# Two chained layers in float32: other loads at the head, and a planner that counts GpSimd's DMAs

## The chip, the cores and the metric

The kernel runs on one core of a Trainium2 chip. The metric is device time in microseconds; of several executions the median is taken. TensorE (PE) does the matmuls, VectorE (DVE) additions and transposes, ScalarE (ACT) scaling and copies, GpSimd (POOL) issues DMAs and SyncE (SP) issues most loads.

## The reference

Eight sequences x[b] of 256 rows by 1024 go through two layers, each added to its input. The first layer is one linear layer plus a masked term; the second picks one of eight weight matrices by an index per sequence:

```python
y = x + (x @ W.T + bias) + (x @ (2 * mask[b] - 1)) * coeff[b]   # mask[b]: 1024 x 1024 of int32
out = y + y @ weight[ids[b]].T                                  # weight[...]: 1024 x 1024
```

All is float32. The mask is 4 MB per sequence, as is the chosen weight. In the first layer both products share x, so the kernel forms one matrix, W.T + coeff * (2 * mask - 1), and multiplies once.

## The kernel before, in words

**Stages.** Layer and sequence make a stage: (0,0), (1,0), (0,1), (0,2), (1,1), (0,3) and so on, 16 in all. Stage (0,0) is the head and is written apart. Every other stage multiplies a 256x1024 by a 1024x1024 matrix with seven block products (Winograd's form of Strassen's scheme): x and the weight are cut into 2x2 blocks, sums s1 to s4 and t1 to t4 are made by DVE (lines 530 and 547), and seven products of 128x512 by 512x512 go into PSUM (line 596; stage 1, which yields the transposed result, uses line 586). Results are added into a buffer r in SBUF by DVE (line 660), some by way of a copy by ACT (line 632).

In a stage of layer 0, each of four mask blocks (1 MB, line 494) is scaled by ACT (`2c * mask - c`, line 503) and folded with W by DVE (line 517). Buffer r begins as the rows of x (line 397), to which a GpSimd DMA adds the bias in flight (line 407). The result is transposed by DVE (line 427) and moved by ACT (line 441) for the second layer. Layer 1 loads its weight blocks from the address that the index gives (line 499); SP reads the index at line 497. Results are stored by GpSimd's queue (line 686). Eleven weight buffers of 1 MB circulate, so a load waits until a buffer is free.

**The head.** Sequence 0 has its 1024 input features in eight groups of 128, k = 0 to 7. For each k, SP loads 128 rows of the mask (`load_mask`, line 267) and of W (`load_w0`, line 274), 512 KB each; k=0 and k=1 come in two column halves (`pieces`, line 248), so there are ten pieces n. Loads of x for this sequence (`load_x0`, line 261; 128 KB per k) go between them in four parts: k=0, k=1, k=2..3, k=4..7. ACT scales a piece (`scale_first`, line 290), DVE adds W (`fold_first`, line 298), and PE multiplies (`mm_first`, line 305), 16 matmuls of 128x256 per k. Piece 0 is scaled and folded in two parts of 256 columns (`parts`). At the end ACT makes x + bias (`bias_first`, line 323) and DVE evicts the four PSUM banks (`evict_first`, line 332). The stage after it starts when these are done.

Three loads of the head, W's first piece (line 785), the index (786) and the coefficients (784), are issued on ACT's queue, and the bias in a layout by partitions (line 278) too, with piece 4. Nine idle matmuls run before the first real one.

**What sets the order.** The order of the whole program is made at build time. Each step is a `Task` with an engine, an estimated length, the tasks it follows, the buffers it takes, and `latest`, a time by which it should start. `plan` is a list scheduler: going through time, it starts on each free engine the ready task with the earliest `latest`. All loads are tasks of one resource "DMA"; stores and bias adds are tasks of POOL, with a length on POOL and a latency. Tasks are then emitted by planned start; every engine runs its own list in that order and waits for the real completions. The estimates are the constants in lines 46 to 48 (PRODUCT is a block product, BLOCK a DVE operation on 128x2048, SMALL one on 128x512, SCALE a mask block on ACT, SHUFFLE a move of line 441), and `HEAD`, 34.5, is where the plan expects the head to end.

Of the kernel before, what the change touches and what calls it, by code (L numbers as in the profile page):

```python
# [14 lines left out]
P = 128  # L15
# [27 lines left out]
}  # L43


PRODUCT, BLOCK, SMALL = 3.435, 2.29, 0.69
SCALE, COPY, SHUFFLE = 2.10, 0.60, 0.42
LOAD, STORE, LATENCY, BEGIN = 2.50, 0.60, 2.2, 1.7


class Task:
    def __init__(
        self, engine, length, emit, after=(), takes=(), uses=(), latency=0.0, latest=None, earliest=0.0
    ):
        self.earliest = earliest
        self.engine, self.length, self.emit = engine, length, emit
        self.after = [t for t in after if t is not None]
        self.takes, self.latency, self.latest = takes, latency, latest
        self.uses = list(takes) + list(uses)
        for r in self.uses:  # L60
            r.users += 1
        self.start = self.end = None
# [9 lines left out]
def plan(tasks, room, may_take):  # L72

    followers = {t: [] for t in tasks}
    for t in tasks:
        for u in t.after:
            followers[u].append(t)
    for t in reversed(tasks):
        due = [f.latest for f in followers[t]]
        own = t.latest + t.length if t.latest is not None else 1e9  # L80
        t.latest = min(due + [own]) - t.length - t.latency
    waiting = {t: len(t.after) for t in tasks}
    ready = {}
    for t in tasks:
        ready.setdefault(t.engine, [])
        if not waiting[t]:
            ready[t.engine].append(t)
    free_at = dict.fromkeys(ready, 0.0)
    free_at["DMA"] = BEGIN
    left = {}  # L90
    events, now, done = [(BEGIN, None)], 0.0, 0
    while done < len(tasks):
        for engine, queue in ready.items():
            if free_at[engine] > now + 1e-9:
                continue
            for t in sorted(queue, key=lambda t: t.latest):
                if t.earliest > now + 1e-9:
                    events.append((t.earliest, None))
                elif all(room[r.pool] > 0 for r in t.takes) and may_take(t):
                    queue.remove(t)  # L100
                    for r in t.takes:
                        room[r.pool] -= 1
                        left[r] = r.users
                    t.start, t.end = now, now + t.length + t.latency
                    free_at[engine] = now + t.length
                    events += [(t.end, t), (free_at[engine], None)]
                    break
        assert events, "the plan is stuck"
        now = min(e[0] for e in events)
        for e in [e for e in events if e[0] <= now + 1e-9]:  # L110
            events.remove(e)
            t = e[1]
            if t is None:
                continue
            done += 1
            for r in t.uses:
                left[r] -= 1
                if not left[r]:
                    room[r.pool] += 1
            for f in followers[t]:  # L120
                waiting[f] -= 1
                if not waiting[f]:
                    ready[f.engine].append(f)
    order = {t: i for i, t in enumerate(tasks)}
    return sorted(tasks, key=lambda t: (round(t.start, 6), order[t]))
# [3 lines left out]
def kernel(  # L129
# [26 lines left out]
    nc = tc.nc  # L156
    B = coeff.shape[1]
    _, _, _, KH, TH = xT.shape
    NL, _, _, _, H = w1T.shape
    KC, D = 2 * KH, 2 * H  # L160
# [84 lines left out]
    first = {(j, h): Buffer("ps") for j in range(2) for h in range(2)}  # L245
    xb = Buffer("r")
    half = KH // 2
    pieces = [(k, ds(j * H, H)) for k in range(2) for j in range(2)]
    pieces += [(k, ds(0, D)) for k in range(2, KC)]
    w0_rows = w0_sb.rearrange("p k j n -> p k (j n)")  # L250

    def x0_view():
# [10 lines left out]
    def load_mask(n: int):  # L263
        k, cols = pieces[n]
        if m[k // 2].tile is None:
            take(m[k // 2])
        nc.sync.dma_start(out=m_view(k)[:, cols].bitcast(I32), in_=mask0[k][:, cols])  # L267
        if n == 0:
            load_x0(0, 1, nc.sync)

    def load_w0(n: int):
        k, cols = pieces[n]
        if n:
            nc.sync.dma_start(out=w0_rows[:, k, cols], in_=w0T[k][:, cols])  # L274
        if n in (1, 3, 5):
            load_x0(*{1: (1, 2), 3: (2, KH), 5: (KH, KC)}[n], nc.sync)
        if n == 4:
            nc.scalar.dma_start(out=b_sb, in_=biasT)

    def parts(n: int):  # L280
        k, cols = pieces[n]
        if n:
            return k, [cols]
        return k, [ds(cols.start, cols.size // 2), ds(cols.start + cols.size // 2, cols.size // 2)]

    def scale_first(n: int):
        k, spans = parts(n)
# [54 lines left out]
    for n, (k, cols) in enumerate(pieces):  # L342
        share = cols.size / D
        opens = opened != k // 2
        length = 1.25 * share if n else 0.4
        ld = task(
            "DMA",
            1.32 * share,
            lambda n=n: load_mask(n),
            takes=[m[k // 2]] if opens else [],  # L350
            uses=[] if opens else [m[k // 2]],
            latency=1.5,
            latest=0.2 * n,
        )
        ld2 = task(
            "DMA", 1.32 * share, lambda n=n: load_w0(n), latency=1.5, latest=0.2 * n + 0.1
        )
        sc = task("ACT", length, lambda n=n: scale_first(n), after=[ld], uses=[m[k // 2]])
        fo = task("DVE", length, lambda n=n: fold_first(n), after=[sc, ld2], uses=[m[k // 2]])
        folded.append(fo)  # L360
        last_scale = sc
        opened = k // 2
        if n == 0:
            tasks[0].takes = [x0] + list(tasks[0].takes)
            tasks[0].uses = [x0] + list(tasks[0].uses)
            x0.users += 1
# [26 lines left out]
    def load_r(b: int, begin: float):  # L393
        task_ = task(
            "DMA",
            LOAD,
            lambda: nc.sync.dma_start(
                out=take(R[b]), in_=xR[b - 1].rearrange("p t (j n) -> p (t j) n", n=H)
            ),
            takes=[R[b]],  # L400
            latency=LATENCY,
            earliest=begin - 8 * PRODUCT,
        )
        return task(
            "POOL",
            1.2,
            lambda: nc.gpsimd.dma_start(  # L407
                out=R[b].tile.rearrange("p (t j) n -> p t (j n)", t=2),
                in_=bias.to_broadcast((P, D)).unsqueeze(1).to_broadcast((P, 2, D)),
                accum_op=ALU.add,  # L410
            ),
            after=[task_],
            uses=[R[b]],
            latency=6.0,
        )

    def turn(j: int, source, after, target: Buffer, opens: bool, view, moved: list):
# [39 lines left out]
    def stage(s: int):  # L457
# [222 lines left out]
        def store(q: str, cols, queue=None):  # L680
            j = int(q[1]) - 1
            lo, hi = j * H + cols.start, j * H + cols.stop
            task(
                "POOL",
                STORE,
                lambda: (queue or nc.gpsimd).dma_start(  # L686
                    out=out0[:, block(q)] if flipped else out[b - 1, :, int(q[0]) - 1, lo:hi],
                    in_=R[b].tile[:, block(q), cols],
                ),
                after=[state[q]],  # L690
                uses=[R[b]],
                latency=3.0,
            )

        copies: dict[str, tuple] = {}
# [86 lines left out]
    with tc.manual_schedule():  # L782
        take(x0)
        nc.scalar.dma_start(out=c_row, in_=coeff)  # L784
        nc.scalar.dma_start(out=w0_rows[:, 0, pieces[0][1]], in_=w0T[0][:, pieces[0][1]])
        nc.scalar.dma_start(out=ids_sb, in_=ids)
        v.memset(zeros, 0.0)
        v.memset(ones, 1.0)
        v.memset(warm, 0.0)

        nc.scalar.activation(warm, warm, AF.Identity, bias=warm, scale=1.0)
        idle = pools["ps"].tile([P, H], F32, tag="ps", name="idle")
        c_ps = pools["ps"].tile([P, B], F32, tag="ps", name="c_ps")
        for n in range(9):
            nc.tensor.matmul(out=idle, lhsT=zeros[:, 0:P], rhs=zeros, start=True, stop=True)
            if n == 4:
                nc.tensor.matmul(out=c_ps, lhsT=ones, rhs=c_row, start=True, stop=True)
                v.tensor_scalar(c2_sb, c_ps, 2.0, None, ALU.mult)
                v.tensor_scalar(cn_sb, c_ps, -1.0, None, ALU.mult)
        for t in plan(tasks, room, may_take):  # L800
            t.emit()
    if DUMP:
        for t in sorted(tasks, key=lambda t: t.start):
            print("PLAN %s %.2f %.2f %.2f" % (t.engine, t.start, t.end, t.latest))
# [55 lines left out]
```

## Time and profile before

| | |
|---|---|
| Time, median of 3 runs | 407.18 us (405.79 to 408.87) |
| The profiled execution's own time | 409.01 us |
| Its span | 407.2 us |
| PE busy in the span | 396.0 us, 97% |
| DVE busy | 329.9 us, 81% |
| ACT busy | 183.4 us, 45% |
| HBM traffic | 94.38 MB read, 8.39 MB written |

The profile is of one execution; 1.8 us of its time lie around the span. A row of waits reads: engine and line, `<-` and what released it, the total in us, the times, the longest. PEld is the loading of PE's stationary operand, which goes on beside the matmuls; a "q" behind an engine is its sequencer, which issues DMAs. In tables by stretches of the span, PEclk is the clock granted to PE, as a share of the full one. "L298" is line 298 of the kernel before.

### The profile page before, as it was taken

How to read it: one execution, taken by the hardware profiler on the slowest of the kernel's cores; microseconds unless marked ns; L12 is line 12 of the kernel's file. 1: busy time of each engine (PE TensorE's matmuls, PEld its weight loads, DVE VectorE, ACT ScalarE, POOL GpSimd, SP SyncE). 2: the span in 40 equal slices, each digit the busy share in tenths (PEclk: the TensorE clock that was granted, in tenths of full speed). 3: DMA queues.
4: the chain of work that ended last, by engine and by line, in shares of the span. 5: the costliest groups of instructions: out<-in, count | busy, mean ns of one | idle time of the engine just before them, and what ended most of it. 6: DMA issues, size and time to landing. Idle time of an engine off the chain costs nothing.

```text
span 407.2 us, 3451 instructions
## 1 busy us (share of the span) xinstructions
PE 396.0 (97%) x1155; PEld 201.6 (50%) x1155; DVE 329.9 (81%) x304; ACT 183.4 (45%) x303; POOL 25.9 (6%) x42
## 2 busy tenths in 40 slices
PE   7699999999999999999999999999999999999996
PEld 4488996443444444444444444444444444444443
DVE  2235999799998998989999898789997899778142
ACT  4234642221992069422966912585128830292000
POOL 0000022001000110001000101001010010001101
PEclk9899999999999999999999999999999999999999
DMA  7999999998872769928599656958679493611102
GB/s 240 362 413 419 423 397 334 348 368 309 208 310 103 283 232 245 375 76 336 207 261 380 215 191 228 334 249 295 244 174 386 154 391 112 241 68 52 53 0 104
DMA packets 18950, 102.99 MB, mean 253 GB/s; under 512 B 2356, under 2 KB 2868, under 8 KB 9460
## 3 DMA queue, kind: packets, MB, share of 16 engines
q1 hardware_dynamic: 14112, 86.97, 54.7%
q0 software_dynamic: 4384, 15.47, 14.6%
q10 hardware_dynamic: 436, 0.33, 0.3%
q8 instruction: 9, 0.15, 0.1%
q14 instruction: 9, 0.07, 0.0%
HBM read 94.38 MB, written 8.39 MB: 252 GB/s over the span
## 4 chain that ended last, share of the span: by engine, by line
PE 87%; DVE 4%; ACT 4%; DMA 3%; issue 1%; SPq 0%; ACTq 0%; DVEq 0%
PE ps L596 75%; PE ps L586 6%; PE ps L305 6%; DMA w_sb<-w0T 3%; ACT a L441 3%; DVE w L547 2%; DVE w L517 1%; DVE r L660 0%; DVE a L530 0%; DVE w L298 0%; ACT u L632 0%; SPq L267 0%; ACTq L784 0%; SPq L274 0%; SPq L261 0%
## 5 line engine op out<-in xcount | busy, mean ns | idle before, releaser
L596 PE MATMUL ps<-w,a 128*128 128x512 f32 (+1 forms) x792 | 337.2, 588 | 1.1 <-DVE a L530 0.7
L596 PEld LDWEIGHTS ps<-w,a 128*128 128x128 f32 x792 | 149.7, 190 | 188.5 <-issue 183.3
L547 DVE TENSOR_TENSOR w<-w,w 128x2048 f32<-128x2048 f32 (+1 forms) x61 | 136.8, 2249 | 7.6 <-PE ps L596 7.2
L441 ACT ACTIVATE a<-turn 32x256 f32<-32x256 f32 x224 | 92.7, 414 | 33.2 <-DVE turn L427 30.5
L503 ACT ACTIVATE w<-w,cn_sb,c_sb 128x2048 f32<-128x2048 int32 x28 | 58.3, 2091 | 21.4 <-DMA w<-mask 20.8
L517 DVE TENSOR_TENSOR w<-w,w_sb 128x2048 f32<-128x2048 f32 x28 | 63.6, 2280 | 4.9 <-ACT w L503 4.9
L660 DVE TENSOR_TENSOR r<-r,ps 128x512 f32<-128x512 f32 x73 | 49.5, 680 | 18.1 <-PE ps L596 17.4
L632 ACT ACTIVATE s<-ps 128x512 f32<-128x512 f32 x15 | 8.9, 592 | 89.6 <-PE ps L596 80.5
L530 DVE TENSOR_TENSOR a<-a 128x512 f32<-128x512 f32 x59 | 39.1, 680 | 0.6 <-ACT a L441 0.5
L305 PE MATMUL ps<-a,w 128*128 128x256 f32 x128 | 29.8, 397 | 5.6 <-DVE w L298 5.6
L686 POOL DMA_DIRECT2D out<-r x31 | 17.5, 565 | 241.0 <-DVE r L660 241.0
L305 PEld LDWEIGHTS ps<-a,w 128*128 128x128 f32 x128 | 25.3, 199 | 10.2 <-DVE w L298 6.5
L632 ACT ACTIVATE u<-ps 128x512 f32<-128x512 f32 x15 | 9.0, 597 | 43.7 <-PE ps L596 43.6
L298 DVE TENSOR_TENSOR w<-w,w_sb 128x1024 f32<-128x1024 f32 (+2 forms) x11 | 10.2, 933 | 18.8 <-DMA w_sb<-w0T 14.1
L586 PE MATMUL ps<-a,w 128*128 128x128 f32 x192 | 21.8, 275 | 0.0
L586 PEld LDWEIGHTS ps<-a,w 128*128 128x128 f32 x192 | 21.7, 192 | 0.1
L427 DVE STREAM_TRANSPOSE turn<-r 128x512 f32<-128x512 f32 x28 | 19.0, 695 | 0.2
L290 ACT ACTIVATE w<-w,cn_sb,c_sb 128x1024 f32<-128x1024 int32 (+2 forms) x11 | 11.0, 1006 | 17.5 <-DMA w<-mask 16.8
L407 POOL DMA_DIRECT2D r<-bias x7 | 8.7, 1247 | 134.8 <-DMA r<-xR 134.8
L660 DVE TENSOR_TENSOR r<-r,u 128x512 f32<-128x512 f32 x14 | 9.6, 686 | 8.3 <-ACT u L632 8.3
L660 DVE TENSOR_TENSOR r<-r,s 128x512 f32<-128x512 f32 x14 | 9.6, 686 | 6.2 <-ACT s L632 6.1
L332 DVE TENSOR_TENSOR a<-ps,r 128x512 f32<-128x512 f32 x4 | 2.7, 687 | 3.4 <-PE ps L305 3.4
(23 smaller groups left out, 23.4 us busy)
## 6 DMA issues: line engine op xcount, KB each, us to landing
w<-w1T SPq DMA_DIRECT2D x32, 1024.0 KB, 8.2
w<-mask SPq DMA_DIRECT2D x28, 1024.0 KB, 9.3
out<-r POOLq DMA_DIRECT2D x31, 256.0 KB, 5.5
a<-xT SPq DMA_DIRECT2D x7, 1024.0 KB, 11.5
r<-xR SPq DMA_DIRECT2D x7, 1024.0 KB, 13.2
r<-bias POOLq DMA_DIRECT2D x7, 1024.0 KB, 11.3
w<-mask SPq DMA_DIRECT2D x6, 512.0 KB, 9.0
w_sb<-w0T SPq DMA_DIRECT2D x6, 512.0 KB, 9.3
```

The lines of the kernel that those rows point to most:

```text
L305: nc.tensor.matmul(out=t.rearrange("p (c n) -> p c n", c=half)[:, c % half], lhsT=m_view(k)[:, ts(oc, P)], rhs=x0_view()[:, k], start=k == ...
L427: lambda t=t, opens=not turned: v.transpose(out=(take(r) if opens else r.tile)[:, t], in_=view(source.tile)[:, 2 * t + j]),
L441: nc.scalar.activation(to[:, :, :, f], src[:, :, :, g], AF.Copy)
L503: nc.scalar.activation(t, t.bitcast(I32), AF.Identity, bias=cn_sb[:, b : b + 1], scale=c2_sb[:, b : b + 1])
L517: lambda q=q: v.tensor_tensor(W[q].tile, W[q].tile, w0[q], ALU.add),
L530: lambda: v.tensor_tensor(part(what), part(left), part(right), op),
L547: v.tensor_tensor(to[:, rows], a, c, op)
L586: nc.tensor.matmul(out=t[:, ts(c, TH)], lhsT=W[w].tile[:, k, ts(c, P)], rhs=part(a)[:, k], start=opens and c == 0 and k == 0, stop=k == KH ...
L596: nc.tensor.matmul(out=t[:, cols], lhsT=part(a)[:, k], rhs=W[w].tile[:, k, cols], start=opens and k == 0, stop=k == KH - 1, skip_group_che ...
L632: lambda: nc.scalar.activation(take(r), bank.tile, AF.Copy),
L660: v.tensor_tensor(to, left, get(r), op)
L686: lambda: (queue or nc.gpsimd).dma_start(out=out0[:, block(q)] if flipped else out[b - 1, :, int(q[0]) - 1, lo:hi], in_=R[b].tile[:, block ...
```

## The change

It has two parts that are independent in the code.

In the head, W's first piece is loaded by SP like the others, and SP's order becomes mask, W, then x where due, for every piece. Only k=0 is still cut into halves: k=1 is one piece of 1024 columns, so nine pieces are left, and `parts` cuts k=1 for ACT and DVE into halves of 512 columns as before. x comes in three loads: k=0..1, k=2..3, k=4..7. The index and the bias are loaded by GpSimd's queue after the first fold: two memsets on DVE, which these loads must wait for, stand behind it. A tenth idle matmul is added.

In the planner, some of the estimates are set anew, the bias add has a longer latency, and a task can have `moves`: a time for which it holds the resource "DMA" when it starts. Bias adds have 4.0 and stores 0.6.

```diff
-PRODUCT, BLOCK, SMALL = 3.435, 2.29, 0.69
-SCALE, COPY, SHUFFLE = 2.10, 0.60, 0.42
+PRODUCT, BLOCK, SMALL = 3.435, 2.21, 0.61
+SCALE, COPY, SHUFFLE = 2.08, 0.60, 0.425
...
                     free_at[engine] = now + t.length
+                    if t.moves:
+                        free_at["DMA"] = max(now, free_at["DMA"]) + t.moves
+                        events.append((free_at["DMA"], None))
...
-    pieces = [(k, ds(j * H, H)) for k in range(2) for j in range(2)]
-    pieces += [(k, ds(0, D)) for k in range(2, KC)]
+    pieces = [(0, ds(0, H)), (0, ds(H, H))] + [(k, ds(0, D)) for k in range(1, KC)]
...
         nc.sync.dma_start(out=m_view(k)[:, cols].bitcast(I32), in_=mask0[k][:, cols])
-        if n == 0:
-            load_x0(0, 1, nc.sync)
...
-        if n:
-            nc.sync.dma_start(out=w0_rows[:, k, cols], in_=w0T[k][:, cols])
-        if n in (1, 3, 5):
-            load_x0(*{1: (1, 2), 3: (2, KH), 5: (KH, KC)}[n], nc.sync)
-        if n == 4:
-            nc.scalar.dma_start(out=b_sb, in_=biasT)
+        nc.sync.dma_start(out=w0_rows[:, k, cols], in_=w0T[k][:, cols])
+        if n in (0, 2, 3):
+            load_x0(*{0: (0, 2), 2: (2, KH), 3: (KH, KC)}[n], nc.sync)
...
-        if n:
-            return k, [cols]
-        return k, [ds(cols.start, cols.size // 2), ds(cols.start + cols.size // 2, cols.size // 2)]
+        size = {0: 2 * P, 2: H}.get(n, cols.size)
+        return k, [ds(at, size) for at in range(cols.start, cols.start + cols.size, size)]
...
-        length = 1.25 * share if n else 0.4
+        length = {0: 0.4, 2: 0.75}.get(n, 1.22 * share)
...
-            latency=6.0,
+            latency=8.5,
+            moves=4.0,
...
                 latency=3.0,
+                moves=0.6,
...
-        nc.scalar.dma_start(out=w0_rows[:, 0, pieces[0][1]], in_=w0T[0][:, pieces[0][1]])
-        nc.scalar.dma_start(out=ids_sb, in_=ids)
...
-        for n in range(9):
+        for n in range(10):
...
             t.emit()
+            if t is folded[0]:
+
+                v.memset(ids_sb, 0)
+                v.memset(b_sb, 0.0)
+                nc.gpsimd.dma_start(out=ids_sb, in_=ids)
+                nc.gpsimd.dma_start(out=b_sb, in_=biasT)
```

More of the change, by code (lines that the diff above doesn't have):

```diff
@@ L52, in __init__ @@
     def __init__(
-        self, engine, length, emit, after=(), takes=(), uses=(), latency=0.0, latest=None, earliest=0.0
+        self,
+        engine,
+        length,
+        emit,
+        after=(),
+        takes=(),
+        uses=(),
+        latency=0.0,
+        latest=None,
+        earliest=0.0,
+        moves=0.0,
     ):
-        self.earliest = earliest
+        self.earliest, self.moves = earliest, moves
         self.engine, self.length, self.emit = engine, length, emit
```

## The prediction

> **What bounds the kernel now.** I read the page's busy rows first: PE is busy 396.0 us of the 407.2 us span, 97%. A time can only come from the other 11 us, or from PE work at a reduced clock. So I asked next where PE idles, by stretches of the span (columns: length, busy time and count of PE, PEld, DVE, ACT, POOL, granted PE clock, DMA share, GB/s):
>
> ```profile
> 0.00:6.87 6.87, 4.12 (x11) 1.45 (x12) 1.13 (x7) 2.67 (x4) 0.20 (x4) 1.00 0.64 205
> 6.87:14.04 7.17, 7.17 (x32) 5.99 (x32) 2.36 (x4) 2.44 (x3) 0.00 (x0) 1.00 0.86 292
> 14.04:18.07 4.03, 0.01 (x2) 0.00 (x1) 1.23 (x1) 1.28 (x2) 0.00 (x0) 1.00 1.03 413
> 18.07:24.00 5.93, 5.93 (x20) 4.93 (x21) 2.01 (x2) 2.44 (x2) 0.00 (x0) 0.71 1.02 409
> ```
>
> PE does no real product before 6.87, then idles 4.03 us, and afterwards runs at 0.71 of its clock for 5.93 us, which costs 5.93 x 0.29 = 1.7 us. In the head, 128 products need 128 x 0.215 = 27.5 us (3.435 us per k, the code's own figure; the first two k took 7.17 here); they take 33.87, from 6.87 to 40.74. The excess of 6.4 is 4.03 + 1.7 + 0.7.
>
> The waits of PE up to 120 us name the cause, and show how little is lost behind the head:
>
> ```profile
> PE ps L305 <- DVE w L298: 5.6, 2, 4.0
> PE ps L596 <- DVE a L530: 0.7, 1, 0.7
> PE ps L596 <- ACT a L441: 0.4, 1, 0.4
> ```
>
> DVE's fold (L298) is late. The chain that ended last, in order of time, says why:
>
> ```profile
> 1.30 4.96 DMA w_sb<-w0T
> ...
> 8.08 8.62 DMA w_sb<-w0T
> ...
> 16.79 1.24 DVE w L298
> ...
> 18.07 22.67 PE ps L305 x96
> ```
>
> Two loads of w0 set the head: the piece on ACT's queue (issued 1.30, landed 6.26) and the one for k=2 (issued 8.08, landed 16.69). Last, what the DMA engines moved in slices of 1.5 us from 0 to 60, and whom SP waited for up to 45:
>
> ```profile
> GB/s 0 223 169 328 384 385 164 178 348 421 408 426 404 415 407 401 426 401 421 418 426 399 431 426 426 426 426 399 431 426 426 426 426 399 410 426 426 431 415 347
> SPq L274 <- DMA a<-x0T: 3.3, 2, 2.4
> SPq L267 <- DMA w_sb<-w0T: 2.5, 2, 2.1
> SPq L274 <- DMA b_sb<-biasT: 1.8, 1, 1.8
> ```
>
> There are two slumps: 3.0 to 4.5 (169) and 9 to 12 (164, 178). Against 385 they lose 1.5 x 216 = 324 KB and 1.5 x (221 + 207) = 642 KB, 0.8 and 1.7 us of transfer. SP holds loads back until older loads have landed, those of ACT's queue included.
>
> **The change, part by part.**
>
> *Loads.* w0's first piece goes second on SP's queue, x0 comes in three pieces instead of four, and k=1 in two 512 KB loads instead of four of 256 KB; index and bias leave ACT's queue. SP issues mask, w0, x0[0:2], mask, w0 and so on, 0.43 us each. SP gains one issue (the w0 piece) and loses three (two of k=1, one of x0), so its issue never becomes the limit: the first eight loads take about 3.5 us to issue and hold 2.6 MB, nearly 7 us of transfer. Are fewer, larger loads worth something in themselves? The trace says little: the four loads of 256 KB for k=1 landed 0.66 us apart (8.53 to 10.51), 397 GB/s; later ones of 512 KB land 1.28 us apart, 410 GB/s. For 1 MB that is 0.1 us. The Trainium skill (DMA: Bandwidth & Descriptors, [...]Issuing engines are not separate DMA queues) speaks against the other half of the edit: moving DMAs between issuing engines saves only issue time. By that rule the first slump stays and the gain is nothing; the nearest row gives 0.8 us, because the slump begins as ACT's piece starts to move, and SP then waits 2.1 us for its landing. I take 0.8, keeping 0 as the other end.
>
> The second slump (1.7 us) has no operation in the trace that explains it. It starts at 9, before the bias load is issued (9.89), and the loads already issued are far from done. It may be a consequence of the first disorder, of the small loads, or of neither. Ends: 0 and 1.7; I take that it goes, since the fixed order has no second queue there, and the 2 KB pieces of k=1 around it are gone.
>
> *Arrivals.* 0.335 MB are moved by 3.0 us (slice of 223 GB/s from 1.5), then 385 GB/s to k=1 and 410 after. Sums: mask, w0, x0[0:2] 0.79 MB at 4.2; half 1 at 5.5; k=1 at 8.3; x0[2:4] and k=2 at 11.5; x0[4:8] and k=3 at 15.3; then 2.56 per k. The last byte of a load lands later than these sums: before, the loads up to w0 of k=1 (2.36 MB) landed at 10.5, little behind the bytes moved, but those of k=5's mask about 2 us behind. I add 1.0 at the front, 1.5 to 2.0 later. Fold (0.69 per half, 1.23 per k) and PE (3.44 per k) then give: first fold 5.3, first product 5.8, k=0 to 9.25; k=1's first half landed 9.4, folded 10.1, PE 10.1 to 13.55; k=2 landed 13.0, folded 14.25, PE to 17.7; k=3 landed 17.0, folded 18.25, PE to 21.7; from k=4 on (landed 19.9) the loads are ahead. Four more k give 35.5, with 0.2 for stalls 35.7. That is 40.74 - 35.7 = 5.0 us earlier. The gaps are 0.85, 0.7 and 0.55. The skill (TensorE: Matmul & The Clock Gate, Part 1) puts the loss of clock after an idle window of about 3.4 us; the trace has one gap over that, 4.03, and 0.71 behind it. So I count no loss of clock; should gaps of this length cost it too, 1.7 returns.
>
> *Scales and folds.* Part sizes remain 256 or 512 columns for k=0 and k=1; the counts are the same, cost nothing. The tenth idle product costs at most 0.43 (nine end at 5.32); hidden before the first fold at 5.3 to 5.7, otherwise 0.4.
>
> *GpSimd's two DMAs.* Two memsets on DVE (0.06 to 0.27 us by the trace's rows, together about 0.2) stand behind the first fold and ahead of the next, which waits for data anyway. GpSimd's issue waits for them, till about 6; its queue is otherwise empty until 54.59. Landing takes 5.5 us (stores) to 11.3 (the bias adds), so 12 to 18. The index is read on SP at 20.96 now, perhaps 17 then: SP could wait 1 us, with some 4 MB queued behind it in the DMA rings, so nothing starves. ACT needs the bias at about 27 (31.98 now): cover of 9 us.
>
> *The planner.* BLOCK 2.21, SMALL 0.61, SHUFFLE 0.425 are what the trace shows as start to start (2.20, 0.60, 13.60 / 32 = 0.425). A store counts 0.6 us and a bias add 4.0 us of DMA; neither adds an instruction, but the order on SP, DVE and ACT may move anywhere. No row can price that. The bounds: behind the head PE loses 0.70 and about 0.44 us in 65.75 to 115.20, and 363.2 us run against some 361.1 of products (7 of stage 1 in 25.0, 98 x 3.43), so at best -2.1; at worst each 128x2048 block that is wrongly placed before something PE needs costs 2.25, because DVE has no air:
>
> ```profile
> 65.75:93.92 28.17, 27.47 (x65) 11.84 (x64) 26.08 (x23) 6.25 (x6) 2.38 (x3) 1.00 1.01 363
> 93.92:115.20 21.28, 20.84 (x48) 8.96 (x48) 20.87 (x20) 13.74 (x34) 1.19 (x1) 1.00 0.83 258
> ```
>
> I take 0.
>
> *What is late next.* In 66 to 115 DVE is 93% and 98% busy and DMA is full to 92. For PE to run 5.0 earlier, both must. DVE's chain starts with the evictions (36.53), which follow PE, and it holds 2.06 us of waiting for PE at 76.7, so it can follow. DMA is ahead by less: at 25.6 it has moved 9.4 MB instead of some 8.25, 2.9 us; the last mask of batch 2 (ACT waits 5.3 for it, scales at 81.95) has a slack of about 1.7 before DVE comes to it. 2.9 + 1.7 = 4.6; together with roughly half a late block I give back 0.8. Sum: 5.0 - 0.8 = 4.2 us. The profiled execution took 409.01 (1.8 around its span), so 404.8 on its own terms; carried as a difference to the median of the runs shown, 407.18, it is **403.0**. Its execution lies at the upper edge of the runs (405.79 to 408.87), so part of the slump may be its own: a reason for a wide upper side.
>
> **Rivals.** Changes within 1% (403.1 to 411.3) can't be told from none here.
> 1. The head closes and the order is harmless: 403.0 (401.3 to 404.8), chance 0.45, over half of it past 1%.
> 2. The head closes and the truer costs also take away the later waits: 5.0 + 1.5 less, 400.7, chance 0.10. For it: the constants match the trace. Against: only 2.1 us exist.
> 3. The change doesn't do what it says: the slump follows the data, not the queue, as the skill's rule has it. k=2 is then 1.7 to 2.5 late, head end about 38.2, and DMA little ahead; gain about 2, 405.1. If the gap passes 3.4 us the clock takes 1.7 more, 406.5. Chance 0.20. For it: a slump that starts with no operation beside it.
> 4. The head closes, but DVE and DMA give it back by 94 us: 406.5, chance 0.08.
> 5. Slower: the planner's new order. Place: DVE between 65 and 115. Price: 2.25 us per block placed ahead of what PE waits for, 1.7 more once PE idles over 3.4. It decides from the second such block on (4.2 used up), and with the clock passes 1% at three (6.75 + 1.7 - 4.2 = 4.25 over, 411.4); four give 413.7. Chance 0.17.
>
> **Numbers.** Faster by over 1%: 0.28 of case 1, 0.10 of case 2, 0.02 of case 3, together 0.40. Slower: 0.17. Within: 0.43. The range 400.4 to 411.5 leaves out about 0.04 below and 0.16 above; the likeliest case alone has 401.3 to 404.8.
>
> **What would show it.** Right: first product near 5.8, no PE gap over 1.5 us before 20, granted clock 1.00 from 18 to 24, head end near 35.7, PE waits of 1 to 2 us somewhere in 65 to 115. Wrong: slices under 250 GB/s between 4 and 13 us (case 3); PE waiting for DVE blocks in stages 2 to 4 (case 5); or a first product later than 6.9 because ten idle products or x0's 256 KB piece hold it.

## The result, and the profile after

The changed kernel takes 405.64 us (median of 20 runs, 404.37 to 406.61) against 406.97 us for the kernel before (20 runs, 405.63 to 408.87). The ratio is 0.9965, 95% interval 0.9952 to 0.9979: 1.3 us are gained, a third of the 4.2 us forecast. The two profiles are of slow executions: 409.01 us lies above all 20 times of the kernel before, and 406.61 us is the highest of the 20 after.

The stretches of the span again, cut at the same times (kernel after; columns as in the prediction's first table):

```profile
0.00:6.87 6.87, 5.08 (x12) 1.65 (x12) 1.56 (x9) 2.67 (x4) 0.85 (x6) 1.00 0.62 154
6.87:14.04 7.17, 5.48 (x13) 4.43 (x14) 1.99 (x3) 2.33 (x3) 0.57 (x2) 1.00 1.04 406
14.04:18.07 4.03, 4.03 (x19) 3.52 (x19) 1.23 (x1) 1.24 (x1) 0.00 (x0) 1.00 1.02 408
18.07:24.00 5.93, 5.93 (x29) 5.21 (x29) 2.45 (x2) 3.02 (x3) 0.00 (x0) 1.00 1.02 409
```

The gap of 4.03 us is gone, and the clock is 1.00 from 18 to 24 as foretold. But the second row holds 13 products where the kernel before had 32. Two things are in it. PE's first real product starts at 8.56 instead of 6.87. And 13 products fill 5.48 us, 0.42 us each, where the row below has 19 in 4.03, 0.21 each: PE runs at half pace. The clock column shows 1.00 there because it has nothing else to show: the trace's first record of a granted clock is at 14.19. One by one, the products from 9.12 to 13.82 start 0.427 us apart, later ones 0.216.

The chain in order of time (kernel after: start, length, what):

```profile
1.68 6.75 DMA a<-x0T
...
8.56 27.20 PE ps L312 x112
```

The first load of x, issued at 1.68, lands at 8.43; the forecast had 5.2. The same load shows in PE's waits, together with all that PE still waits for behind the head:

```profile
PE ps L312 <- DMA a<-x0T: 2.3, 1, 2.3
...
PE ps L594 <- DVE a L538: 0.2, 1, 0.2
```

What the DMA engines moved, in slices of 1.5 us from 0 to 60 (kernel after):

```profile
GB/s 0 232 197 116 317 403 415 403 408 421 399 412 415 396 418 410 407 429 399 431 421 421 431 410 421 431 421 415 426 415 426 431 410 415 421 415 333 314 306 284
```

Of the two slumps one is left, and it is where it hurts most: 197 and 116 from 3 to 6 us, just when the first product's data should come. From 7.5 us on the stream is full.

So the head ends later than forecast: stage 1's products start at 39.04 (before: 40.58). Behind it the span has 365.8 us left, where the kernel before had 366.6. The stretches in which DVE was thought to have no air (kernel after):

```profile
66.00:94.00 28.00, 28.00 (x66) 12.37 (x66) 27.06 (x23) 8.07 (x6) 1.78 (x2) 1.00 0.89 326
94.00:115.00 21.00, 21.00 (x50) 9.31 (x49) 20.86 (x23) 17.22 (x35) 1.23 (x1) 1.00 0.52 210
```

DVE is still 97% and 99% busy, but PE has no gap any more.

### The profile page after: what moved, and what is told of

The parts are those of the page before. It is cut to its first block, busy times and chain, and to the rows that moved or that the text cites. A ratio compares the mean times of both kernels' runs of the same rounds, so it can differ in the third digit from the quotient of the medians.

```text
span 404.8 us, 3432 instructions
## 1 busy us (share of the span) xinstructions
PE 397.5 (98%) x1156; PEld 203.0 (50%) x1156; DVE 330.6 (82%) x306; ACT 183.5 (45%) x303; POOL 27.2 (7%) x44
## 4 chain that ended last, share of the span: by engine, by line
PE 95%; DMA 2%; DVE 1%; issue 1%; SPq 0%; DVEq 0%
PE ps L604 83%; PE ps L312 7%; PE ps L594 5%; DMA a<-x0T 2%; DVE w L555 1%; DVE a L339 0%; DVE a L538 0%; SPq L283 0%; SPq L279 0%; DVE r L753 0%; DVEq L339 0%
## 5 line engine op out<-in xcount | busy, mean ns | idle before, releaser
L312 PEld LDWEIGHTS ps<-a,w 128*128 128x128 f32 x128 | 26.2, 206 | 7.2 <-issue 3.2
L594 PEld LDWEIGHTS ps<-a,w 128*128 128x128 f32 x192 | 21.8, 192 | 0.5 <-DVE a L538 0.4
```

The lines of the kernel that those rows point to most:

```text
L312: nc.tensor.matmul(out=t.rearrange("p (c n) -> p c n", c=half)[:, c % half], lhsT=m_view(k)[:, ts(oc, P)], rhs=x0_view()[:, k], start=k == ...
L594: nc.tensor.matmul(out=t[:, ts(c, TH)], lhsT=W[w].tile[:, k, ts(c, P)], rhs=part(a)[:, k], start=opens and c == 0 and k == 0, stop=k == KH ...
```

## The experiments

The pitch of x is the distance in DRAM from the start of one of its 128 rows to the start of the next. All ratios are to the kernel before, run on the same chip, where its median was 406.76 to 407.45. "x lands" is the landing of the first load of x (k=0 and 1; with the head of the kernel before k=0 alone, 128 KB), "stage 1" the start of the next stage's products, both in the one profiled execution.

| run | what differs | median us | ratio (95%) | x lands | stage 1 |
|---|---|---|---|---|---|
| before | | 406.97 | 1 | 6.07 | 40.58 |
| after | | 405.64 | 0.9965 (0.9952 to 0.9979) | 8.43 | 39.04 |
| e1_planner_only | planner's part alone | 406.05 | 0.9974 (0.9959 to 0.9990) | 5.47 | 37.24 |
| e2_head_only | head's part alone | 406.80 | 0.9986 (0.9970 to 1.0003) | 6.77 | 37.25 |
| e3_x0_contiguous | after, x contiguous | 404.09 | 0.9927 (0.9898 to 0.9955) | 5.83 | 36.35 |
| e4_no_first_x0 | after, no first load of x | 403.56 | 0.9909 (0.9873 to 0.9945) | none | 36.15 |
| e5_before_x0_contiguous | before, x contiguous | 405.00 | 0.9945 (0.9921 to 0.9969) | 4.94 | 35.82 |
| e6_padded_pitch | after, pitch 9472 B | 403.84 | 0.9918 (0.9888 to 0.9949) | 6.29 | 36.21 |
| e7_after_16_idle | after, 16 idle products | 405.57 | 0.9959 (0.9938 to 0.9980) | 8.24 | 38.05 |
| e8_contiguous_fill | e3, idle products between | 404.13 | 0.9919 (0.9887 to 0.9951) | 6.08 | 36.67 |
| e9_old_head_padded | before's head, planner, pitch 9472 B | 403.91 | 0.9926 (0.9897 to 0.9955) | 5.42 | 37.99 |
| e10_padded_small_x | e6, first x load in two | 404.09 | 0.9919 (0.9893 to 0.9946) | 5.90 | 36.69 |
| e11_pitch_16k | after, pitch 16384 B | 404.60 | 0.9930 (0.9904 to 0.9956) | 5.29 | 36.86 |
| e12_after_again | after | 405.83 | 0.9972 (0.9959 to 0.9986) | 7.97 | 38.65 |
| e13_rows_behind | after, 20 unread rows behind x | 405.35 | 0.9955 (0.9935 to 0.9975) | 8.51 | 38.73 |
| e14_rows_ahead | after, 20 unread rows ahead of x | 406.00 | 0.9967 (0.9952 to 0.9981) | 8.34 | 38.40 |
| e15_padded_again | e6 | 404.01 | 0.9917 (0.9889 to 0.9945) | 6.26 | 36.80 |

**The two parts apart.** The kernel before with only the constants, the latency of 8.5 and `moves`; and the kernel after without these.

```diff
# e1_planner_only, on the kernel before
+PRODUCT, BLOCK, SMALL = 3.435, 2.21, 0.61
+SCALE, COPY, SHUFFLE = 2.08, 0.60, 0.425
...
+            latency=8.5,
+            moves=4.0,
...
+                moves=0.6,
# e2_head_only, on the kernel after: the same lines as in the kernel before
```

> The planner's part alone, on the kernel before; the head stays as it was. Theory A (the two parts add up, each gives part of the 1.3 us: the trace of after lost 1.0 us less behind the head): ratio 0.997 to 0.998, head end at 40 to 41 us as before, 362 us behind it instead of 363.2. Rival B (the planner's part gives nothing by itself, the later waits vanished for other reasons): 0.9995 to 1.0005. Rival C (the new order costs and hides a larger gain of the head): over 1.002.

> The head's part alone, with the old constants and without moves. Theory A: head end at about 39.2 us as in the trace of after, ratio 0.998 to 0.999. Rival B: the head gives all, 0.9965. Rival C: 0.993 or less, about 404.2 us and under.

Theory A fits: 0.9974 and 0.9986, about 1.3 and 0.6 us, and the product of the two ratios, 0.996, is near the 0.9965 of the whole change. The planner's part looks the larger, but the intervals overlap and the head's reaches past 1. From the start of stage 1 to the end of the span there are 365.9 us with it (e1) and 367.0 without (e2), against 365.8 in the kernel after and 366.6 in the one before.

The head ends expected were missed in both, and it matters: 37.25 instead of 39.2 in e2, and e1 has the head of the kernel before, and yet its stage 1 starts at 37.24, not at 40 to 41. Its PE rows and its slices (e1):

```profile
6.43 9.16 PE L309 MATMUL ps<-a,w 128*128 128x256 f32 x32 [0.57 <-DVE w L302]
16.42 20.99 PE L309 MATMUL ps<-a,w 128*128 128x256 f32 x96 [0.83 <-DVE w L302]
```

```profile
GB/s 0 225 146 332 395 396 249 253 419 415 416 415 407 412 410 407 412 421 418 421 415 410 437 431 426 404 421 415 437 426 426 404 415 410 437 421 391 306 309 298
```

The same two slumps are there, but the second is shallower (249 and 253 instead of 164 and 178), the gap before k=2 is 0.83 us instead of 4.02, and no clock is lost behind it (it is granted at 10.47, so that the first 32 products take 9.16 us). SP's order of loads in the head is that of the kernel before, so the end of one and the same head differs by 3.3 us between these two executions; the one profiled of e1, 404.94 us, was the fastest of its 22.

**Is it x?** In the trace of after, the slump begins when the first load of x has its turn, and SP's issues become slow in it (1.0 us instead of 0.4):

```profile
3.09 0.43 SPq L279 DMA_DIRECT2D w<-mask  x1
3.56 1.04 SPq L283 DMA_DIRECT2D w_sb<-w0T  x1
4.65 1.06 SPq L273 DMA_DIRECT2D a<-x0T  x1
```

Two theories: the load itself, whose rows of 2 KB lie 8 KB apart in DRAM; or the burst of issues on SP. First x is laid out anew, with nothing else changed; then its first load is taken away, which leaves x of k=0 and 1 out of the result.

```diff
# e3_x0_contiguous
-        queue.dma_start(out=x0_view()[:, lo:hi], in_=x0T[:, lo:hi])
+        src = {0: x0A, 2: x0B, KH: x0C}[lo]     # three arrays: x0[:, 0:2], x0[:, 2:KH], x0[:, KH:]
+        queue.dma_start(out=x0_view()[:, lo:hi], in_=src)
...
# e4_no_first_x0
-        if n in (0, 2, 3):
+        if n in (2, 3):
...
+        v.memset(x0_view()[:, 0:2], 1.0)
```

> The kernel after, with x of sequence 0 kept in DRAM as three arrays, so that the rows of each of its three loads lie one behind the other (2 KB rows at a pitch of 2 KB instead of 8 KB); same loads, same order, same bytes. Theory X (the slump of the DMA, now at 3.5 to 6.5 us, comes with the first load of x, because of the 8 KB pitch): no slice under 300 GB/s from 3 to 8 us, first x lands at about 5.2 instead of 8.4, first product near 6 us, head end near 36 us, ratio to before 0.988 to 0.991. Rival Y (it comes from a burst of issues on SP while many loads are on their way, whatever they read): x lands at 8.4 as before, no change against after, ratio 0.9965.

> The kernel after without the first load of x (k=0 and 1 of sequence 0 are filled with ones by DVE instead, so x of these features is left out of the first product and the residual). 256 KB less to load. Theory X: no slump at all from 3 to 8 us, or a short one at the second load of x (also 2 KB of an 8 KB pitch); first product 5.5 to 6 us, ratio 0.987 to 0.991. Rival Y: SP still issues its loads as fast, so the slump stays at 3.5 to 6.5 us, the second half of k=0 lands after 8 us, and the ratio is 0.993 to 0.996 (first product early, then a wait).

Their slices, of e3 and of e4:

```profile
GB/s 0 240 216 340 335 403 417 374 418 415 415 415 404 412 407 412 410 418 423 421 426 421 426 410 431 421 421 426 415 421 431 410 415 421 421 328 289 309 317 306
```

```profile
GB/s 0 262 190 306 397 322 258 416 419 412 410 412 412 407 410 407 415 415 429 421 421 421 421 421 431 421 415 421 421 426 426 415 404 426 415 369 300 306 306 306
```

With contiguous rows the slice from 4.5 to 6 has 340 instead of 116; a dip to 216 before it remains, so the expected "none under 300" is missed there. x lands at 5.83, 2.6 us sooner, and the time falls by about 1.5 us (the ratio, 0.9927, is a little short of the 0.988 to 0.991 expected). Without the first load the hole at 3 to 6 is smaller (190, 306), and a new one opens at 7.5 to 10.5 (322, 258), where the second load of x comes, again 2 KB of each 8 KB. In both, SP's first seven issues begin at the same times as in the kernel after, the seventh at 3.56; the burst is not it. The slow issues go with the slump: the eighth, begun at 4.04, takes 0.66 us in e3 and, right behind x's load, 0.97 in e4.

**The kernel before has it too.**

```diff
# e5_before_x0_contiguous, on the kernel before
-        queue.dma_start(out=x0_view()[:, lo:hi], in_=x0T[:, lo:hi])
+        src = {0: x0A, 1: x0B, 2: x0C, KH: x0D}[lo]   # four arrays, one for each load
+        queue.dma_start(out=x0_view()[:, lo:hi], in_=src)
...
# e9_old_head_padded: e1, with x as in e6
```

> The kernel before, unchanged but for x of sequence 0, kept in DRAM as four arrays, one for each of its loads, so that rows lie one behind the other. Theory X (the first loads of x at a pitch of 8 KB make the slump, in the kernel before too): no slice of 1.5 us under 250 GB/s from 4.5 to 13 us, k=2's load of w0 lands at 12.5 to 13.5 instead of 16.7, head end 36.5 to 38 us, ratio to before 0.990 to 0.994, about as much as the contiguous form gained on the kernel after; then the order of the loads and SP's queue are worth little once x is contiguous. Rival Y (in the kernel before the two queues and the small loads make the slump, x has nothing to do with it): 0.999 to 1.001.

> The head of the kernel before (ACT's queue, ten pieces, x in four loads), with the planner's part of the change and with x at the pitch of 9472 B. Theory N (once the pitch is mended, the new order of the head's loads is worth nothing): ratio 0.991 to 0.993, the same as the kernel after at this pitch (0.9918), head end 35.5 to 36.5 us. Rival M (the new order is worth its 0.6 us there too): 0.9935 to 0.995.

```profile
GB/s 0 197 250 371 387 344 288 406 418 409 423 396 415 412 407 418 404 418 421 434 410 415 431 426 415 437 404 415 431 431 410 426 404 415 431 426 410 371 300 314
```

In e5 the second slump, 164 and 178 from 9 to 12 us in the kernel before, is 344 and 288 from 7.5 to 10.5; k=2's load of W lands at 13.6 instead of 16.7 (it was to be 13.5 at most). Against the kernel before on the same chip (407.08) 2.1 us are gained with the old order and ACT's queue in place; the ratio, 0.9945, is just outside the 0.990 to 0.994 expected. And e9, old head, new planner, mended pitch, takes 403.91 with the ratio 0.9926; the new head at that pitch has 0.9918 and 0.9917. The intervals overlap: once x is laid out otherwise, no worth of the new order of loads can be measured. One expectation of e9 was missed: its head ends at 37.99 instead of 35.5 to 36.5 in the profiled execution, where PE idled 2.02 us ahead of k=2 and the clock was then at 0.50 from 16.07 to 19.48.

```profile
6.28 7.17 PE L309 MATMUL ps<-a,w 128*128 128x256 f32 x32 [0.42 <-DVE w L302]
15.48 22.68 PE L309 MATMUL ps<-a,w 128*128 128x256 f32 x96 [2.02 <-DVE w L302]
```

**The pitch, or the place?** The rows of x stay scattered, at other pitches; then the pitch stays and the array moves.

```diff
# e6_padded_pitch (and e15_padded_again); e11_pitch_16k has 2048 for 320
+    x0 = np.pad(x0, ((0, 0), (0, 320)))         # x0: 128 rows of 2048 numbers
...
# e13_rows_behind; e14_rows_ahead has (20, 0) and reads rows 20 to 147
+        "x0T": np.pad(x[0].reshape(S, 2 * KH, P).transpose(2, 1, 0), ((0, 20), (0, 0), (0, 0))),
+        queue.dma_start(out=x0_view()[:, lo:hi], in_=x0T[0:0+P, lo:hi])
...
# e10_padded_small_x, on e6
+            load_x0(*{0: (0, 1), 1: (1, 2), 2: (2, KH), 3: (KH, KC)}[n], nc.sync)
```

> The kernel after, with the rows of x for sequence 0 still scattered in DRAM, but at a pitch of 9472 B instead of 8192 B (each row is padded by 1280 B that are never read). Theory P (the pitch of 8 KB, a power of two, sets it): first load of x lands before 6.5 us and the ratio is that of the contiguous form, 0.991 to 0.994. Theory S (that the rows are scattered, not the exact pitch): x lands at 7 to 8.5 us, ratio 0.996 to 0.998.

> The kernel after with the rows of x at a pitch of 16384 B instead of 8192 B (padding that is never read). Theory P (a power-of-two pitch sets the slump; twice the pitch puts the rows on the same few places or fewer): first load of x lands at 8.4 us or later, up to 11; ratio 0.9965 to 1.003. Rival (8 KB was an accident of addresses, any other pitch is good): x lands before 6.5 us, ratio 0.991 to 0.993.

> The kernel after, once more, beside the next three on the same chip. If its slump at the first load of x is a property of the kernel: a slice under 200 GB/s between 3 and 6 us, x lands at 6.5 to 8.5 us, ratio 0.9952 to 0.998. If it was a property of the executions seen so far: x lands before 6.3, ratio under 0.994.

> The kernel after with x of sequence 0 at its pitch of 8192 B, in an array of 148 rows whose last 20 are never read: arrays that follow it in memory (the masks of the head among them, if they are laid one behind the other) move by 160 KB against it. Theory P (the pitch of 8 KB itself): slump as in the kernel after, x lands at 6.5 to 8.5 us, ratio 0.9955 to 0.998. Rival L (where x lies against the masks): x lands before 6.3 us, ratio 0.991 to 0.994.

> As the run before, with the 20 unread rows ahead of those read: x moves by 160 KB against W, which comes before it, and keeps its place against the masks. Theory P: slump as in the kernel after, ratio 0.9955 to 0.998. Rival L2 (where x lies against W, or its own address): x lands before 6.3 us, ratio 0.991 to 0.994.

> The pitch of 9472 B once more, on the chip of the three others. If the gain of the padded pitch over the kernel after is real: 1.2 to 2.0 us under the kernel after on the same chip, x lands before 6.5 us.

> The kernel after with x at the pitch of 9472 B, and its first load of x cut into k=0 and k=1 again (128 KB each, the second behind piece 1), so that 128 KB less stand ahead of the first product. If the bytes ahead bound it: first product 0.3 us sooner (6.1 instead of 6.4), second half of k=0 too, ratio 0.9905 to 0.9918. If the folds of k=1 and 2 bound the head anyway: 0.9918, no change.

The slices of e6, pitch 9472 B:

```profile
GB/s 0 257 202 287 303 411 408 404 415 407 415 410 404 412 412 401 418 412 429 426 410 431 421 421 421 431 410 426 421 426 415 426 404 421 415 410 300 309 319 292
```

Of e11, pitch 16384 B:

```profile
GB/s 0 249 238 273 333 396 373 411 412 418 407 412 404 418 410 404 418 415 423 421 415 426 426 421 426 410 426 426 421 426 421 410 415 426 415 371 300 303 311 295
```

And of e13, pitch 8192 B, with rows behind:

```profile
GB/s 0 242 178 82 274 412 415 404 410 407 412 407 412 410 410 412 404 415 421 423 421 415 421 431 426 415 421 421 415 437 426 415 415 410 415 426 339 303 311 289
```

At 9472 B the slice from 4.5 to 6 has 287, at 16384 B 273, at 8192 B 82 to 127 (e12, and e13 and e14 with the array moved by 160 KB against its neighbours). On one chip, the padded pitch takes 404.01 us against 405.83, 405.35 and 406.00 for the three at 8192 B. So the pitch does it, and not scattering as such; nor does the place, as far as these two shifts can tell. That twice the pitch is good too refutes what I expected of powers of two; why 8192 B is bad and 16384 B is not stays open. Cutting the first load of x (e10) brings the first product forward to 6.04, but the second group still starts at 8.77, for want of its fold: no gain.

**The half pace.**

```diff
# e7_after_16_idle
-        for n in range(10):
+        for n in range(16):
# e8_contiguous_fill, on e3: behind both halves of k=0 and behind k=1
+                for _ in range(2):
+                    nc.tensor.matmul(out=idle, lhsT=zeros[:, 0:P], rhs=zeros, start=True, stop=True)
```

> The kernel after with 16 idle products ahead of the first real one instead of 10, so that PE stays busy until about 8 us, when x lands; nothing else. Theory H (in the trace of after 12.5 products from 8.56 to 13.82 us run 0.427 us apart instead of 0.2145, half the clock, because PE had idled from 6.28 to 8.56 and the full clock had not been granted; that costs 2.6 us of the head in such an execution): first products 0.2145 us apart at the latest from 8.6 us, ratio to before 0.993 to 0.995. Rival (the pace is not what bounds the head, the loads are next right behind): ratio 0.9955 to 0.998.

> The contiguous form of after with two idle products behind each of the first three groups of real ones (both halves of k=0, and k=1), where PE waits 0.7, 0.7 and 0.2 us for folds. Theory H (the moment at which the full clock is granted differs between executions, and small gaps at the start put it off): ratio 0.990 to 0.992, the spread of times under 1 us. Rival: 0.9925 to 0.994, no better than the contiguous form, since the idle products only fill time in which nothing is granted, or delay the real ones by 0.2 to 0.4 us.

PE's rows in e7:

```profile
3.97 3.67 PE L802 MATMUL idle<-zeros 128*128 128x512 bf16 x11
8.38 1.97 PE L312 MATMUL ps<-a,w 128*128 128x256 f32 x8 [0.73 <-DMA a<-x0T]
10.55 1.99 PE L312 MATMUL ps<-a,w 128*128 128x256 f32 x8 [0.21 <-DVE w L305]
13.11 25.10 PE L312 MATMUL ps<-a,w 128*128 128x256 f32 x112 [0.57 <-DVE w L305]
```

The first eight products now take 1.97 us, full pace from the start, and PE waits for folds instead: the rival was right that the loads are next right behind. (The full pace that the expectation puts at 0.2145 us is 0.216 in the traces.) Stage 1 starts 1.0 us sooner in the profiled execution, but the median, 405.57, is that of the kernel after. e8's time is that of e3; its interval holds both expectations, so it tells nothing.

## Why the prediction was wrong

- **"I take that it goes"**, said of the second slump, is the step that failed. It rested on two companions of the slump, ACT's queue and the 2 KB pieces of k=1. With the order and ACT's queue kept and x alone laid out anew (e5), the slump shrinks to 344 and 288 and 2.1 us are gained; so the layout of x was the cause, and by its time the slump is that of the third load of x, x[2:4], with rows of 2 KB at a pitch of 8 KB. A row that the prediction shows pointed there: of `SPq L274 <- DMA a<-x0T: 3.3, 2, 2.4`, the 2.4 us run from 11.71 to 14.09, right behind the slump, to the landing of x[2:4]. The change made such a load the third of all, so the slump moved from 9 to 12 us to 3 to 6. The first slump, counted as 0.8 us, did not go either (197 GB/s against 169). Two of the signs that the prediction named for being wrong came true: slices under 250 GB/s between 4 and 13 us, and a first product later than 6.9, at 8.56, that waits for x's piece of 256 KB. Rival 3, "the slump follows the data, not the queue", was the case, at a chance of 0.20. That its 405.1 is 0.5 from the measured time is in part luck: it has 2 us from the head and none from the planner, where the runs have about 0.6 and 1.3.
- **Arrivals.** From k=1 on the sums were fair: w0 of k=2 landed at 15.74 instead of 13.0, the slump's 2.7 us late. With the pitch mended (e6) it landed at 13.63, the first product started at 6.42 (5.8 forecast) and stage 1 at 36.21 (35.7). The working was sound but for the slump.
- **"I count no loss of clock".** PE idled 2.3 us before the first product, less than the 3.4 us that the Trainium skill states (TensorE: Matmul & The Clock Gate, Part 1), and yet ran at half pace up to the product at 13.82; in e14 and e9 a clock already granted was withdrawn after gaps of 2.26 and 2.02 us, so the measurement decides against that use of the rule. In the kernel after no clock was withdrawn: none had been granted before 14.19, and the prediction had taken a full clock at the first product for given. That is 12.5 x 0.211 = 2.6 us of PE time, most of it over waits for loads that it would have had anyway: e7 without it gains 1.0 in the profile and nothing that can be measured in the median. First product 2.76 late, 2.6 of half pace, less the 2.3 of gaps in the forecast that vanished: 3.1 us, nearly all of the difference between 35.7 and 39.04.
- **"The planner: I take 0"**, and 0.8 given back. The planner's part is worth 1.3 us (0.9974), with an interval up to 0.9990. Nothing was given back: from stage 1 to the end there are 365.8 us after a head that ends at 39.04 (after) and at 36.35 (e3). With the old planner there is a sign of it: 366.6 us after a head that ends at 40.58 (before), 367.5 after 35.82 (e5). Rival 5, the new order as a loss, did not happen. DVE's busy share, 93 and 98% in the prediction's rows and 97 and 99% after, had said "no air"; it did not mean that PE must wait.
- **The base.** The 5.0 us of the head were taken from one execution with a gap of 4.03 and a clock withdrawn behind it, and carried to the median. How common such an execution is, the mean granted clock of each run tells: of 47 runs of the kernel before on one chip, 13 have 0.996 or less, as the profiled one has, and their median is 408.54 us; the other 34 have 406.38. The note that it lay "at the upper edge" was right, and should have cut the sum and not only widened the range. An estimate of the typical head, from the medians less 1.8 us around the span and less the time behind the head in the profiles (366.6 and 365.8): it ends near 38.6 before and near 38.0 after. Of the 5.0 forecast, 2.0 were then the base, 2.3 the slump and the slow start (38.0 against 35.7), and 0.6 was gained, which is what e2 has.
- **Right:** the stream full behind 9 us and the clock at 1.00 from 18 to 24; the two GpSimd DMAs at no cost (the index landed at 11.5, the bias at 11.9; nobody waited); and nothing measurable gained from fewer loads as such. That PE has no gap behind k=0 was luck: the half pace gave the loads time to get ahead, and e7, at full pace, has gaps of 0.21 and 0.57.

The best version found is e6, the kernel after with 1280 B of padding in each row of x: 403.84 and 404.01 us, ratios 0.9918 and 0.9917, some 1.8 us faster than the kernel after on the same chip. The contiguous form (e3) and the old head with the same padding (e9) can't be told from it.

## What to carry to other kernels

When transfers stall with loads still queued, look at the layout in DRAM of the load that has its turn before blaming queues: 1280 unread bytes in each row of 8192 did more here than a new order of all the head's loads. A profile is one execution: compare its own time, and its granted clock, with those of the other runs before taking a gap in it for the average gap. And a full DVE ahead of a full PE says nothing yet about who waits; only the wait rows do.

## What the runs showed of the hardware

- A load of 128 rows of 2 KB at a pitch of 8192 B went with a slump of all DMA traffic: 82 to 132 GB/s for 1.5 us where 400 are usual, in each of the six profiled executions with the new head and this pitch. At 9472 B and 16384 B the same bytes passed at 236 to 287. A second such load soon after the first, as in the kernel after, did no visible harm; in e4, with the first one gone, the second did (258). Where in the memory it jams can't be told from these traces.
- The granted clock was recorded in steps of 3.41 us (e14: granted at 6.01, withdrawn at 9.42, granted at 12.84), at a phase that differs between executions. It was withdrawn though PE had idled only 2.26 us, from 6.21 to 8.47, and had worked for the rest of that step. In e9 a gap of 2.02 us, from 13.45 to 15.48, cost it too; in the kernel before one of 1.55 us, from 5.32 to 6.87, did not. If the steps run on backwards from the first grant, PE had worked in the kernel after for some 68% and 65% of the two steps from 3.95 to 10.78, and was granted nothing until a full one had passed. The rows of e14, with the granted clock third from the end:

```profile
6.01:9.42 3.41, 1.15 (x6) 0.87 (x6) 0.00 (x0) 0.13 (x1) 1.22 (x2) 1.00 0.96 372
9.43:12.83 3.40, 3.40 (x10) 2.57 (x9) 0.81 (x2) 2.19 (x3) 0.00 (x0) 0.50 1.03 406
```

- Before the first record the profile's clock column says 1.00 whatever the clock is; the spacing of the products tells (0.427 against 0.216 us).
